# Edge attention on one core: batches of eight tiles in place of four

## The chip, the core and the metric

The kernel runs on one core of one Trainium2 chip. The core has TensorE (PE, with its weight loads PEld), VectorE (DVE), ScalarE (ACT), GpSimd (POOL) and SyncE (SP), which run at once, each through its own instructions in order. A queue instruction (SPq, ACTq, POOLq in the profile) loads registers or starts a transfer. The metric is device time in microseconds (us). Three runs of the kernel before took 2592.5, 2565.03 and 2586.32 us; the median is 2586.32 us.

## What is computed

A graph attention layer with 6250 nodes and 206250 edges, 128 features in 8 heads of 16, then a residual and a layer norm. The edges are sorted by destination.

```python
Qh = (h @ WQ).reshape(N, H, D); Kh = (h @ WK)...; Vh = (h @ WV)...
Eh = (edge_attr @ WE).reshape(-1, H, D)
score = einsum('ehd,ehd,ehd->eh', Kh[src], Qh[dst], Eh) / sqrt(16)
score = exp(clip(score, -5.0, 5.0))
wV = segment_sum(Vh[src] * score[:, :, None], dst)
Z  = segment_sum(score, dst)
x  = layernorm(x + wV / (Z[:, :, None] + 1e-06))
```

All is float32 in and out.

## The kernel before

**Tiles and batches.** 128 edges make a tile, one edge to a partition; there are NT = 1612 tiles. Four tiles make a batch (B = 4), 406 batches with the short ones at the end (`cut_batches`). The loop at L580 runs once for each batch b and issues one stage of batch b, another of b-1 and a third of b-2:

- `stage_a(b)` on PE: L464 forms Q of the batch's edges from a one-hot matrix (`onehotT`) and rows of Q, into the one `qps` buffer; L469 forms E from the edge attributes `ea` into the one `eps` buffer. Each buffer is one PSUM bank (4 x 128 floats). A buffer is free again when DVE has read it.
- `stage_b(b-1)` on DVE: `kq` = K x Q (L475), `kqe` = kq x E (L478), the sum by heads `sc` (L481), the clip (L484). Between these lie, for a batch to come, the one-hot matrices `onehot` (L437, reads `iota_p` in PSUM) and `onehotT` (L450), both made for two batches at a time, and calls of `fill`, each of which issues one instruction of the waiting layer norms or of the waiting rows of Q.
- `weigh(b-1)` on ACT: exp of the scores twice, into `exp_p` in PSUM (L490) and into the tail of `msg` (L492).
- `messages(b-2)` on DVE: msg = V x exp_p (L519).
- `stage_c(b-2)` on PE: L541 adds onehot x msg into `agg`, a window of 64 nodes; eight tiles share one window. Two windows share a PSUM tile, which ACT copies out in one piece (`sum`, L552).

**K and V by two ways.** Before the loop a table `kv` of K and V of all nodes is made. For each tile POOL starts an indirect transfer (`gather`, L397) of 128 rows of it into `kvrows`. The first transfer of batch b waits for the Q matmuls of batch b - lag(b) (L401); the rest of the batch follow it. One tile in ten takes another way instead: `columns` (L370) copies its nodes' columns of x, one after another at addresses held in registers, 96 of 128 on ACT and 32 on DVE. The addresses are loaded eight at a time from `col_at` (L365). When a column tile `xcol` is complete, PE multiplies it (L379, `colkv`) and DVE places the result (L386). On ACT a batch's copies stand in two halves, one before `weigh` and one after it; on DVE they stand behind `messages` and ahead of the clip. `COLP` sets the rate: a column tile in every 5/2 batches, from batch COL0 = 32 on, started COLL batches ahead. There are 146 such tiles and 14016 copies on ACT.

**Order.** From batch XB = 12 on the order on each engine is that of the program. SP's queue holds the loads of `ea` (8 tiles each, three such chunks ahead), of `relb`, of the rows of Q (`qw`), and the stores. The batches before 12 gather rows of x and form K and V by `project`.

Of the kernel before, what the change touches and what calls it, by code (L numbers as in the profile page):

```python
# [16 lines left out]
P = 128  # L17
N, E, D, H, DH = 6250, 206250, 128, 8, 16
NT = (E + P - 1) // P
EPAD = NT * P  # L20
B = 4
G = 4
# [6 lines left out]
CH = 8  # L29
GB = 14  # L30
XB = 12
LOCK = XB + 6
STEP = 3
GLEAD = 2
OHB = 5
# [4 lines left out]
NG = (NT + G - 1) // G  # L40
AHEAD = 2
EB = 6
SLAG = 2
WT = 8
# [6 lines left out]
QREG = 16  # L51
COL0 = 32
COLP = (5, 2)
COLA = (8, 12)
COLV = (8, 4)
COLL = 8
RING = 4096
SUMS = 8
XT_AT = RING + P
# [3 lines left out]
def cut_batches():  # L63
    out, t = [], 0
    while t < NT:
        k = B
        if t >= NT - TAIL:
            k = 2 if NT - t > 3 else 1
        out.append(range(t, t + k))
        t += k  # L70
    return out
# [30 lines left out]
def edge_attention(ctx: ExitStack, tc: tile.TileContext, x, xT, srcT, srcC, dstT, dstB, dst0, bnd, lo, eaT,  # L102
# [25 lines left out]
    ident = cp.tile([P, P], F32, name="ident")  # L128
    onehots = [cp.tile([P, HW + 2 * B * P], F32, name=f"onehot{i}") for i in range(OHB)]
    cnt_i = cp.tile([1, 1], I32, name="cnt_i")  # L130
# [10 lines left out]
    with ExitStack() as fast:  # L141
# [98 lines left out]
        psT = fast.enter_context(tc.tile_pool(name="psT", bufs=2, space=bass.MemoryType.PSUM))  # L240
        psA = fast.enter_context(tc.tile_pool(name="psA", bufs=2, space=bass.MemoryType.PSUM))
# [106 lines left out]
        used = [0]  # L348

# [58 lines left out]
        def project(g, n):  # L408

            pt = psT.tile([P, B, P], F32, name="xtps", tag="oT")  # L410
            for i in range(n):
                nc.tensor.transpose(pt[:, i, :], g[:, i, :D], ident)
            xgT = wp.tile([P, B, P], F32, name="xgT", tag="kq", bufs=2)
            nc.scalar.copy(xgT[:, :n], pt[:, :n])
            for i in range(0, n, 2):
                k = min(2, n - i)
                pk = pair_bank(i // 2, "kvps", [P, 2, 2 * D])
                for j in range(k):
                    nc.tensor.matmul(pk[:, j, :], xgT[:, i + j, :], wkv_sb, start=True, stop=True)  # L419
                nc.scalar.copy(g[:, i:i + k, :], pk[:, :k, :])  # L420

        def together(b):

            t0 = batches[b][0]
            n = len(batches[b])
            if n == B and b + 1 < nbat and len(batches[b + 1]) == B and t0 % (2 * B) == 0:
                return [b, b + 1]
            return [] if n == B and t0 % (2 * B) else [b]

        def stage_0(b):  # L430
            group = together(b)
            if not group:
                return
            t0, n = batches[b][0], sum(len(batches[i]) for i in group)
            tl = onehots[used[0] % OHB]
            used[0] += 1
# [3 lines left out]
            for i in group:  # L440
                st8[i] = tl, HW + (batches[i][0] - t0) * P - HW * pair_of(batches[i][0])[1], None

        def stage_0t(b):
            group = together(b)
            if not group:
                return
            t0, n = batches[b][0], sum(len(batches[i]) for i in group)
            ohT = wp.tile([QROWS, 2 * B * P], BF16, name="onehotT", bufs=3)
# [3 lines left out]
            for i in group:  # L452
                tl, at, _ = st8[i]
                k = (batches[i][0] - t0) * P
                st8[i] = (tl, at), ohT[:, k:k + len(batches[i]) * P]

# [15 lines left out]
        def stage_b(b):  # L472
            n, g, oh, pq, pe = st8[b]
            t0 = wp.tile([P, B, D], F32, name="kq", bufs=2)
            nc.vector.tensor_tensor(t0[:, :n], g[:, :n, :D], pq[:, :n], op=ALU.mult)  # L475
            yield
            t1 = wp.tile([P, B, D], F32, name="kqe", bufs=2)
            nc.vector.tensor_tensor(t1[:, :n], t0[:, :n], pe[:, :n], op=ALU.mult)  # L478
            yield
            sc = wp.tile([P, B, H], F32, name="sc")  # L480
            nc.vector.tensor_reduce(sc[:, :n], t1[:, :n].rearrange("p b (h d) -> p b h d", h=H),  # L481
                                    axis=AX.X, op=ALU.add)
            yield
            nc.vector.tensor_scalar(sc[:, :n], sc[:, :n], -20.0, 20.0, op0=ALU.max, op1=ALU.min)  # L484
            st8[b] = [n, g, oh, sc]

        def weigh(b):

            n, g, oh, sc = st8[b]
            nc.scalar.activation(exp_p[:, :n], sc[:, :n], AF.Exp, scale=0.25)  # L490
            m = wp.tile([P, B, MW], F32, name="msg")
            nc.scalar.activation(m[:, :n, D:], sc[:, :n], AF.Exp, scale=0.25)  # L492
# [7 lines left out]
        def add_windows(ps, q, first, stop):  # L500

            parts = windows(q)
            for i, (k, s) in enumerate(parts):
                nc.tensor.matmul(ps, shift[:, P - s:2 * P - s], sums[k // 2][:, k % 2],  # L504
                                 start=first and i == 0, stop=stop and i == len(parts) - 1)
# [18 lines left out]
        def stage_c(b):  # L524
            n, g, oh, m = st8.pop(b)
            for i in range(n):
# [6 lines left out]
                final = k == NT  # L533
                u = k if final else k // 2
                first = u not in aggs
                if first:
                    aggs[u] = psA.tile([P, 2, MW], F32, name="agg")
                    if final:
                        add_windows(aggs[u][:, 0], QL, True, False)
                tail = k == NT if t == NT - 1 else pair_of(t + 1)[0] != k  # L540
                nc.tensor.matmul(aggs[u][:, 0 if final else k % 2], oh[0][:, oh[1] + i * P:oh[1] + i * P + P], m[:, i, :],  # L541
                                 start=not final and t % (2 * G) == 0, stop=tail)
                if tail and final:
# [3 lines left out]
                    while norms:  # L547
                        fill()
                    norms.append(layernorm(nc, sp, aggs.pop(u)[:, :1], xbs.pop(QL), out, QL, 1, stores))
                elif tail and (k % 2 == 1 or t == LAST - 1):  # L550
                    sums[u] = sp.tile([P, 2, MW], F32, name="sum", bufs=SUMS)
                    nc.scalar.copy(sums[u][:, :k % 2 + 1], aggs.pop(u)[:, :k % 2 + 1])  # L552
                    while len(finished) < QL // 2 and all(v // 2 <= u for v, _ in windows(2 * len(finished) + 1)):
                        ready.append(len(finished))
                        finished.append(u)

        gathered = {b: gather(b) for b in range(2)}
        for b0 in range(0, NB, KB):
# [3 lines left out]
            for b in range(len(gathered), min(XB, nbat)):  # L562
                if (b - 2 if b < 5 else b) * KB > b0:
                    break
# [20 lines left out]
        for b in range(nbat + 3):  # L585
# [7 lines left out]
            if b < nbat:  # L593
# [4 lines left out]
                if b == min(XB, nbat - 1):  # L598
                    late_loads()
                if b == min(XB + 8, nbat - 1):  # L600
                    relative(C0, NT)
                if b == 14:
                    from_window(1)
# [38 lines left out]
            if b < nbat:  # L642
                project_columns(b + GLEAD)
                build_q(q_built(min(NJ - 1, batches[b][0] // WT + QLOOK + 2)), True)
                if not qwork and len(built) < q_built(
                        min(NJ - 1, batches[min(nbat - 1, b + 4)][0] // WT + QLOOK + 2)):
# [3 lines left out]
            if b == min(60, nbat):  # L650
                count_inside()
            if b == min(80, nbat + 1):
                inside = nc.values_load(cnt_i[0:1, 0:1], min_val=0, max_val=2 * EPAD,
# [159 lines left out]
```

## Time and profile before

The profiled execution took 2567.26 us, of which the span, from the first to the last instruction, is 2565.4 us.

| What | Value | Where from |
|---|---|---|
| Profiled execution / span | 2567.26 / 2565.4 us | result and page |
| Loads of column addresses: ACT / DVE | 1752 / 584 | the view of L365 |
| Granted TensorE clock | 0.75 | result |
| DMA | 148 GB/s on average, 380.81 MB | page, part 2 |
| First and last load of column addresses on ACT | 251.8 and 2489.9 us | the view of L365 |
| One load of eight addresses on ACT / DVE | 555 / 606 ns median | the same |
| `kqe`, `sc` (128 x 512) | 676, 672 ns each | groups by line |
| exp into `exp_p` (128 x 32) | 193 ns | the same |
| copy of two windows, `sum` (128 x 272) | 374 ns | the same |

A group's time is from an instruction's start to its end; neighbours on one engine overlap, so that a run of copies of 189 ns each starts one every 95 ns. "Idle before" is the time that the engine stood still ahead of the group, and behind it stands what ended that: an instruction of another engine, or "issue", which is idle time for which the profile shows no wait.

### The profile page before, as it was taken

Reading aid. Unit: us, or ns where it says so; the run is one execution under the profiler, and the core shown is the slowest. Engines: PE = TensorE matmul, PEld = TensorE weight load, DVE = VectorE, ACT = ScalarE, POOL = GpSimd, SP = SyncE. Lnnn points to the kernel's source line nnn. Section 1 sums busy time; section 2 is a strip of 40 time slices with the busy share of each in tenths; the row PEclk is TensorE's granted clock in tenths of the full one; section 3 lists DMA queues with packets and bytes.
Section 4 is the critical chain, followed back from the end, with each engine's and each line's share of the span. In section 5 each row is a group of like instructions: output and inputs, shape, how many; then the busy total and the mean of one; then the engine's idle time right before and its main releaser. Section 6 shows DMA issues by size and latency. Waiting matters only on the chain.

```text
span 2565.4 us, 49832 instructions
## 1 busy us (share of the span) xinstructions
PE 1624.0 (63%) x9342; PEld 1407.1 (55%) x9342; DVE 1843.5 (72%) x8070; ACT 1644.0 (64%) x15015; POOL 1396.9 (54%) x1473
## 2 busy tenths in 40 slices
PE   5656566676666666666666655667666656566665
PEld 3446555565665555555555555556556555455555
DVE  2436678878777777777767777877877777777786
ACT  1211667777776677676767767777776666776760
POOL 6446555555555455555554555555655555555564
PEclk7777777777776777776777768777876777777787
DMA  7545445645554464455444544564654455545542
GB/s 233 153 130 179 136 125 157 176 134 169 153 148 132 134 176 138 123 147 174 130 135 136 175 140 129 147 175 137 183 147 126 136 144 164 145 131 144 173 145 79
DMA packets 171028, 380.81 MB, mean 148 GB/s; under 512 B 58653, under 2 KB 84569, under 8 KB 170707
## 3 DMA queue, kind: packets, MB, share of 16 engines
q0 software_dynamic: 69584, 189.03, 25.8%
q1 hardware_dynamic: 99983, 187.46, 24.4%
q14 instruction: 244, 2.00, 0.2%
q8 instruction: 77, 1.26, 0.2%
q10 hardware_dynamic: 1140, 1.06, 0.1%
HBM read 362.61 MB, written 14.81 MB: 147 GB/s over the span
## 4 chain that ended last, share of the span: by engine, by line
ACT 46%; issue 25%; DVE 11%; PE 8%; ACTq 6%; another core or an unknown queue 3%; DMA 1%; DVEq 0%; SPq 0%
ACT xcol L370 42%; ACTq L365 6%; DVE xcol L370 2%; PE agg L541 2%; PE eps L469 2%; ACT msg L492 2%; DVE kqe L478 2%; DVE msg L519 1%; DVE kq L475 1%; PE finps L504 1%; ACT exp_p L490 1%; PE kvps L419 1%; DVE sc L481 1%; ACT sum L552 1%
## 5 line engine op out<-in xcount | busy, mean ns | idle before, releaser
L397 POOL DMA_INDIRECT kvrows<-kv,src x1418 | 1350.3, 952 | 1120.4 <-PE qps L464 420.4
L370 ACT COPY xcol<-xT_sb 128x4 uint8 x14016 | 1499.0, 189 | 573.0 <-issue 560.3
L541 PE MATMUL agg<-msg,onehot 128*128 128x136 f32 x3224 | 639.1, 358 | 441.3 <-DVE msg L519 316.8
L541 PEld LDWEIGHTS agg<-msg,onehot 128*128 128x128 f32 x3224 | 562.4, 254 | 492.2 <-ACT msg L492 276.5
L469 PE MATMUL eps<-we_sb,ea 128*128 128x128 f32 x3224 | 599.6, 343 | 164.5 <-DVE kqe L478 95.3
L469 PEld LDWEIGHTS eps<-we_sb,ea 128*128 128x128 f32 x3224 | 517.8, 244 | 220.6 <-DVE kqe L478 128.7
L519 DVE TENSOR_TENSOR msg<-kvrows,exp_p 128x512 f32<-128x512 f32 x406 | 275.9, 679 | 488.8 <-ACT exp_p L490 276.4
L370 DVE COPY xcol<-xT_sb 128x4 uint8 x4672 | 410.9, 192 | 30.2 <-issue 23.0
L464 PE MATMUL qps<-qw,onehotT 126*128 126x128 bf16 x1612 | 193.5, 254 | 240.7 <-DVE kq L475 163.2
L464 PEld LDWEIGHTS <-onehotT 126*128 126x128 bf16 x1612 | 154.7, 117 | 325.3 <-issue 306.8
L478 DVE TENSOR_TENSOR kqe<-kq,eps 128x512 f32<-128x512 f32 x406 | 274.6, 676 | 52.3 <-remote 30.7
L475 DVE TENSOR_TENSOR kq<-kvrows,qps 128x512 f32<-128x512 f32 x406 | 273.7, 674 | 37.5 <-remote 21.3
L481 DVE TENSOR_REDUCE sc<-kqe 128x32 f32<-128x512 f32 x406 | 272.8, 672 | 5.8 <-DVE y L761 0.5
L490 ACT ACTIVATE exp_p<-sc 128x32 f32<-128x32 f32 x406 | 78.3, 193 | 139.7 <-DVE sc L484 76.8
L437 DVE TENSOR_TENSOR onehot<-iota_p,dst_sb 128x512 f32<-128x512 f32 (+2 forms) x206 | 137.6, 669 | 11.0 <-remote 9.0
L379 PE MATMUL colkv<-wkv_sb,xcol 128*128 128x256 f32 x292 | 127.9, 533 | 0.0
L504 PE MATMUL finps<-sum,shift 128*128 128x136 f32 x640 | 95.2, 310 | 17.1 <-ACT sum L552 11.1
L504 PEld LDWEIGHTS finps<-sum,shift 128*128 128x128 f32 x640 | 91.1, 219 | 19.6 <-ACT sum L552 13.1
L492 ACT ACTIVATE msg<-sc 128x32 f32<-128x32 f32 x406 | 87.2, 215 | 22.2 <-issue 21.7
L450 DVE TENSOR_SCALAR onehotT<-relb,node 126x1024 bf16<-126x1024 bf16 (+2 forms) x206 | 99.8, 485 | 1.8 <-DMA relb<-relD 1.7
L484 DVE TENSOR_SCALAR sc<-sc 128x32 f32<-128x32 f32 x406 | 83.7, 206 | 4.2 <-issue 3.8
L379 PEld LDWEIGHTS colkv<-wkv_sb,xcol 128*128 128x128 f32 x292 | 69.1, 285 | 0.0
(73 smaller groups left out, 568.9 us busy)
## 6 DMA issues: line engine op xcount, KB each, us to landing
ea<-eaT SPq DMA_DIRECT2D x201, 512.0 KB
relb<-relD SPq DMA_DIRECT2D x100, 504.0 KB
kvrows<-kv,src POOLq DMA_INDIRECT x1418
qw<-qs SPq DMA_DIRECT2D x202, 31.5 KB
kv<-kvst SPq DMA_DIRECT2D x12, 512.0 KB
qs<-qst SPq DMA_DIRECT2D x48, 96.0 KB
xb<-x SPq DMA_DIRECT2D x24, 128.0 KB
out<-h SPq DMA_DIRECT2D x24, 128.0 KB
```

The source lines that it names most:

```text
L365: at = nc.values_load_multi_w_load_instructions(col_at[k % col_half:k % col_half + 1, k // col_half, j:j + size], engines=(engine,), min_v ...
L370: copy(to[:, 4 * (j + c):4 * (j + c) + 4], xT_bytes[:, ds(at[c] - XT_AT, 4)])
L379: nc.tensor.matmul(pk, col_tiles.pop(k), wkv_sb, start=True, stop=True)
L397: ins = nc.gpsimd.indirect_dma_start(out=g[:k, i, :f], out_offset=None, in_=rows, in_offset=bass.IndirectOffsetOnAxis(ap=src_col(t)[:k], a ...
L464: expanded[b] = nc.tensor.matmul(pq[:, i, :], ohT[:, i * P:i * P + P], loaded[t0 // WT], start=True, stop=True)
L469: nc.tensor.matmul(pe[:, i, :], ea[:, i * P:i * P + P], we_sb, start=True, stop=True)
L475: nc.vector.tensor_tensor(t0[:, :n], g[:, :n, :D], pq[:, :n], op=ALU.mult)
L478: nc.vector.tensor_tensor(t1[:, :n], t0[:, :n], pe[:, :n], op=ALU.mult)
L481: nc.vector.tensor_reduce(sc[:, :n], t1[:, :n].rearrange("p b (h d) -> p b h d", h=H), axis=AX.X, op=ALU.add)
L504: nc.tensor.matmul(ps, shift[:, P - s:2 * P - s], sums[k // 2][:, k % 2], start=first and i == 0, stop=stop and i == len(parts) - 1)
L519: nc.vector.tensor_tensor(m[:, :n, :D].rearrange("p b (h d) -> p b h d", h=H), g[:, :n, D:].rearrange("p b (h d) -> p b h d", h=H), exp_p[ ...
L541: nc.tensor.matmul(aggs[u][:, 0 if final else k % 2], oh[0][:, oh[1] + i * P:oh[1] + i * P + P], m[:, i, :], start=not final and t % (2 * ...
```

## The change

Eight tiles make a batch (206 batches). E and Q of a batch take two PSUM banks each, still one buffer each. To find the banks, `iota_p` and `exp_p` become two parts of one tile `bank`, and the window sums `agg` become one tile for the whole kernel, in whose two halves the windows alternate; ACT copies each window by itself (136 wide). `kqe` is written over `kq`; `sc` and `msg` have two buffers. `onehot` and `onehotT` are made for each batch by itself, which is eight tiles as before. Seven calls of `fill` stand in an iteration where four did. The gathers, the look-ahead and the column rate are scaled, a column tile falling on 6/5 batches of eight, 9.6 tiles. By the code there are 150 of them.

```diff
-B = 4
+B = 8
-GB = 14
-XB = 12
-LOCK = XB + 6
-STEP = 3
-GLEAD = 2
+GB = 8
+XB = 6
+LOCK = XB + 3
+STEP = 2
+GLEAD = 1
-AHEAD = 2
-EB = 6
-SLAG = 2
+AHEAD = 1
+EB = 5
+SLAG = 1
-COL0 = 32
-COLP = (5, 2)
+COL0 = 16
+COLP = (6, 5)
-COLL = 8
+COLL = 5
-SUMS = 8
+SUMS = 16
...
-        iota_p = psX.tile([P, HW], F32, name="iota_p")
-        exp_p = psX.tile([P, B, H], F32, name="exp_p")
+        bank = psX.tile([P, HW + B * H], F32, name="bank")
+        iota_p, exp_p = bank[:, :HW], bank[:, HW:].rearrange("p (b h) -> p b h", h=H)
+        agg = psA.tile([P, 2, MW], F32, name="agg")
...
-            return max(STEP, 12 - (b - LOCK) // 40)
+            return max(STEP, 6 - (b - LOCK) // 20)
...
-            t1 = wp.tile([P, B, D], F32, name="kqe", bufs=2)
+            t1 = t0
-            sc = wp.tile([P, B, H], F32, name="sc")
+            sc = wp.tile([P, B, H], F32, name="sc", bufs=2)
-            m = wp.tile([P, B, MW], F32, name="msg")
+            m = wp.tile([P, B, MW], F32, name="msg", bufs=2)
...
+                nc.tensor.matmul(agg[:, u % 2], oh[:, i * P + HW - HW * half:][:, :P], m[:, i, :],
                                  start=not final and t % (2 * G) == 0, stop=tail)
...
+                elif tail:
+                    sums[k] = sp.tile([P, MW], F32, name="sum", bufs=SUMS)
+                    nc.scalar.copy(sums[k], agg[:, k % 2])
...
             fill()
+            fill()
             next(steps, None)
             if b + AHEAD < nbat:
                 stage_0t(b + AHEAD)
+            fill()
             fill()
...
             if b < nbat:
                 columns(nc.vector, b)
+            fill()
             fill()
```

More of the change, by code (lines that the diff above doesn't have):

```diff
@@ L128, in edge_attention @@
     ident = cp.tile([P, P], F32, name="ident")
-    onehots = [cp.tile([P, HW + 2 * B * P], F32, name=f"onehot{i}") for i in range(OHB)]
+    onehots = [cp.tile([P, HW + B * P], F32, name=f"onehot{i}") for i in range(OHB)]
     cnt_i = cp.tile([1, 1], I32, name="cnt_i")
@@ L408, in project @@
         def project(g, n):
[L410 to L428, printed above, removed]
-        def stage_0(b):
[L431 to L436, printed above, removed]
+            for a in range(0, n, G):
+                h = min(G, n - a)
+                pt = psT.tile([P, G, P], F32, name="xtps", tag="oT")
+                for i in range(h):
+                    nc.tensor.transpose(pt[:, i, :], g[:, a + i, :D], ident)
+                xgT = wp.tile([P, G, P], F32, name="xgT", tag="kvst", bufs=2)
+                nc.scalar.copy(xgT[:, :h], pt[:, :h])
+                for i in range(0, h, 2):
+                    k = min(2, h - i)
+                    pk = pair_bank(i // 2, "kvps", [P, 2, 2 * D])
+                    for j in range(k):
+                        nc.tensor.matmul(pk[:, j, :], xgT[:, i + j, :], wkv_sb, start=True, stop=True)
+                    nc.scalar.copy(g[:, a + i:a + i + k, :], pk[:, :k, :])
+        def stage_0(b):
+            t0, n = batches[b][0], len(batches[b])
+            tl = onehots[b % OHB]
             nc.vector.tensor_tensor(tl[:, HW:].rearrange("p (t n) -> p t n", n=P)[:, :n, :HW],
@@ L439, in stage_0 @@
                                     rel[:, t0:t0 + n, None].to_broadcast([P, n, HW]), op=ALU.is_equal)
-            for i in group:
-                st8[i] = tl, HW + (batches[i][0] - t0) * P - HW * pair_of(batches[i][0])[1], None
+            st8[b] = tl, None
         def stage_0t(b):
[L444 to L448, printed above, removed]
+            t0, n = batches[b][0], len(batches[b])
+            ohT = wp.tile([QROWS, B * P], BF16, name="onehotT", bufs=2)
             e0 = t0 % RC * P
@@ L451, in stage_0t @@
                                     op0=ALU.is_equal)
[L452 to L455, printed above, removed]
+            st8[b] = st8[b][0], ohT
         def stage_a(b, g):
@@ L548, in stage_c @@
                         fill()
[L549 to L553, printed above, removed]
+                    norms.append(layernorm(nc, sp, agg[:, u % 2:u % 2 + 1], xbs.pop(QL), out, QL, 1, stores))
+                elif tail:
+                    sums[k] = sp.tile([P, MW], F32, name="sum", bufs=SUMS)
+                    nc.scalar.copy(sums[k], agg[:, k % 2])
+                    while len(finished) < QL // 2 and all(v <= k for v, _ in windows(2 * len(finished) + 1)):
                         ready.append(len(finished))
-                        finished.append(u)
-        gathered = {b: gather(b) for b in range(2)}
+                        finished.append(k)
+        gathered = {0: gather(0)}
         for b0 in range(0, NB, KB):
@@ L562, in edge_attention @@
             for b in range(len(gathered), min(XB, nbat)):
-                if (b - 2 if b < 5 else b) * KB > b0:
+                if (2 * b - 1 if b < 3 else 2 * b + 1) * KB > b0 and b0 + KB < NB:
                     break
```

31 lines of the change are left out of this document (13 added, 18 removed).

## The prediction, made before the changed kernel was run

> **What bounds the kernel now.** I read the page first: the busy times, the chain that ended last, the costliest groups.
>
> ```profile
> PE 1624.0 (63%) x9342; PEld 1407.1 (55%) x9342; DVE 1843.5 (72%) x8070; ACT 1644.0 (64%) x15015; POOL 1396.9 (54%) x1473
> ...
> ACT 46%; issue 25%; DVE 11%; PE 8%; ACTq 6%; another core or an unknown queue 3%; DMA 1%; DVEq 0%; SPq 0%
> ...
> L370 ACT COPY xcol<-xT_sb 128x4 uint8 x14016 | 1499.0, 189 | 573.0 <-issue 560.3
> ```
>
> DVE is busiest, but the chain runs through ACT: 46% ACT's own work, nearly all column copies, 25% "issue". The copies take 1499.0 us and 573.0 us of standing still ahead of them, together 2072 us of the 2238 us between ACT's first and last column load (251.8 and 2489.9). Next the view of waits: who is late?
>
> ```profile
> ACT xcol L370 <- issue: 560.3, 1033, 1.2
> DVE msg L519 <- ACT exp_p L490: 276.4, 151, 6.1
> ACT exp_p L490 <- DVE sc L484: 76.8, 22, 18.7
> ```
>
> DVE waits for ACT's exp (276.4 us), ACT for DVE's scores much less, and in the column stretch only 10.5 us. So ACT's stream of copies sets the pace there: 2238 us / 14016 = 159.7 ns a copy, everything included.
>
> **What makes ACT stand.** In the timeline ACT's idle "issue" time comes in phases, and they lie in the later part of POOL's runs of gathers. A run is a row of gathers with 0.3 us between them, 1.25 us each. The view by stages, for column copies alone, over a run of three (from 1003.08), one of four (1007.81), one of eight (1052.01 to 1061.78) and one of seven (1068.09 to 1076.66):
>
> ```profile
> core 0: us, PE busy (x) PEld busy (x) DVE busy (x) ACT busy (x), PEclk, DMA share, GB/s
> 1003.00:1006.00 3.00, 0.00 (x0) 0.00 (x0) 0.95 (x12) 2.63 (x28) 1.00 0.94 269
> 1006.00:1007.80 1.80, 0.00 (x0) 0.00 (x0) 0.54 (x7) 0.84 (x9) 1.00 0.75 189
> 1007.80:1010.80 3.00, 0.00 (x0) 0.00 (x0) 1.54 (x16) 2.84 (x30) 0.80 0.25 71
> 1010.80:1013.70 2.90, 0.00 (x0) 0.00 (x0) 0.00 (x0) 1.16 (x10) 0.50 0.42 124
> ...
> 1052.00:1055.00 3.00, 0.00 (x0) 0.00 (x0) 1.39 (x16) 2.84 (x30) 0.83 0.86 244
> 1055.00:1062.80 7.80, 0.00 (x0) 0.00 (x0) 0.00 (x0) 2.19 (x16) 0.50 0.42 123
> 1062.80:1068.10 5.30, 1.06 (x2) 0.56 (x2) 0.67 (x8) 4.34 (x45) 0.54 0.04 15
> 1068.10:1071.10 3.00, 0.00 (x0) 0.00 (x0) 1.34 (x16) 2.82 (x30) 1.00 0.23 57
> 1071.10:1077.70 6.60, 0.00 (x0) 0.00 (x0) 1.81 (x16) 1.92 (x13) 0.76 0.37 104
> ```
>
> The first 3 us of every run carry about 30 ACT copies, full rate. After that the rate falls to about 2 per us (16 in 7.8 us, 13 in 6.6 us) until 1 us after the run, and a pause of 0.9 us ahead of the run at 1052 was enough to give full rate again. The DMA share does not order these rows (0.86 in a fast one, 0.42 in the slowest). Counted over all runs from 300 to 2450 us, copies started per us, by the us since the run began: runs of four (136 of them) 9.1, 9.1, 8.4, 3.5, 3.1, 3.3; of seven (40) 9.5, 9.2, 8.6, 3.0, 3.2, 2.1, 0.4, 2.6, 1.8, 1.7, then 9.5; of eight (15) 8.7, 10.0, 9.9, 3.4, 3.1, 1.7, 0.5, 2.3, 1.7, 1.5, 1.3, 6.7, then 9.7. From the start of one run to that of the next, between 600 and 2400 us: 5.30 us after a run of three (76 cases), 6.23 of four (104), 13.96 of seven (38), 15.56 of eight (14). Two batches fetched apart take 11.5 us, fetched in one run 14 to 15.6.
>
> **The change part by part.**
>
> *Gathers.* A batch's gathers follow one trigger. Seven (eight where the batch has no column tile) will now always make one run; today this is so in 55 of 287 runs. An iteration has 14400/180 = 80 ACT copies. In five of six iterations a run of seven: 42.1 copies in 10 us by the row above, the other 37.9 at 9.5 per us, 14.0 us. In the sixth a run of eight: 50.8 copies in 12 us and 29.2 at 9.7, 15.0 us. POOL is busy 9 to 10 us of these, so the next run stays apart.
>
> *Exps and window copies on ACT.* In the timeline a pair of exps costs ACT 0.25 us from start to next start. From the exp of 32 (193 ns) to the copy of 272 (374 ns) is 0.76 ns an element, so a pair of 64 costs 0.30 and replaces two: -0.20 us an iteration. Two copies of 136 for one of 272 cost +0.07 per two iterations. Net -0.165 us, within bounds of -0.25 and 0. The iteration: (5 x 13.8 + 14.85)/6 = 14.0 us.
>
> *DVE.* No row shows these products at 1024 elements from two banks; nearest is a tensor_tensor of 128x1024 in SBUF at 1224 ns and a reduce at 1212. So kq, kqe, sc and msg save 4 x (2 x 0.675 - 1.22) = 0.5 us per eight tiles, and between 0 and 0.7; a clip less saves 0.2. It's hidden: DVE waits for ACT. The Perfetto Trace Analysis page of the Trainium skill (Optimizing Scalar/DVE Operations) says that larger operations help where the engine is saturated, and that smaller ones may be better where it isn't and makes bubbles elsewhere. By the first half of it 0.7 us an iteration would come off the end; DVE's 72% speaks for the second.
>
> *A new wait.* `iota_p` and `exp_p` now share a tile, and in the built program `onehot` waits for ACT's exp; before, only msg did. Behind it in DVE's queue stand kqe, onehotT, sc, msg, the placing, the column copies and the clip, and for the clip ACT's next exp waits. That chain by the rows: 0.67 + 1.22 + 0.49 + 1.21 + 1.22 + 0.35 + 26.7 x 0.088 + 0.21, 0.88 for layer norm and Q rows, 0.3 for the exp: 8.9 us. It runs beside ACT's 14.0, with 5 us to spare: nothing.
>
> *PE, SP, the rest.* E and Q of eight tiles wait for kq and kqe as before, half as often; PE is 63% busy and off the chain: nothing. The agg matmuls now wait for ACT's copy of the window before, which stands about 40 copies behind the exp, and msg also comes late: 0 to 2 us, on PE alone. SP's stores of Q rows hold its queue up to 30 us (its waits in 1000:1400), with `ea` loaded two chunks (28 us) ahead and SP itself running ahead: PE waited 1.8 us for `ea` in that stretch, so 0, at most some us for each of 49 stores, and PE has room. In-place kqe: no instruction more or less.
>
> *Ends.* Columns begin at tile 96 as now (252 us). The start I leave alone: same table, same 48 projected tiles, bounds -10 and +15. The last ACT copy falls in iteration 192, leaving 76 tiles where 56 take 75 us today (2490 to 2565): 102 us.
>
> Sum: 252 + 180 x 14.0 + 102 = 2874 us of span, against 252 + 2238 + 75 = 2565; with the 1.9 us around it 2876. The profiled execution (2567.26) lies 0.7% under the median of the runs; halfway gives **2890**.
>
> **Rivals.**
>
> *Run length is not the cause, faster.* Long runs and slow ACT might have a third cause. If eight tiles then cost what two short cycles do, 11.53, plus 3.2 copies more (0.3), less 0.165: 11.7 us, 252 + 2106 + 102 = 2460. For it: one long run replaces two triggers and the chain of 8.9 us would allow it. Against: the slow rows end with the run, 191 runs of both lengths agree on the first 6 us, and the idle time is no semaphore's. The Runtime: NRT & Kernel Launch page of the Trainium skill (Instruction fetch mechanics) has engines fetch their instructions by themselves, mostly hidden; by it ACT would be fed evenly and this case would hold. The 560.3 us of issue speak against it.
>
> *Issue loss goes with the number of copies, not with runs.* 14400 x 159.7 ns = 2300, less 180 x 0.165: 2270; 252 + 2270 + 102 = 2624, slower by 2%. For: ACT's program is hardly changed. Against: 11.5 and 14 us for the same work.
>
> *The new wait closes a loop on DVE, far slower.* DVE's copies fall 7 to 9 us into a run; there its steps grew from 83 to 150 to 205 ns. At 205 the chain has 12.0 us, hidden. At ACT's slow rate (0.45 us) 26.7 copies add 9.7: 18.6 us an iteration, 3700. It decides from 14.0 us on, when 14 of the copies are that slow. Against: DVE's copies stood for issue only 23 us in all.
>
> **How the numbers follow.** Forecast 0.70, its iteration 13.4 to 14.8 us, so 2770 to 3020; faster 0.12; loss by copies 0.13; the DVE loop 0.05. The range 2600 to 3030 takes in the forecast and the loss by copies and leaves out the others, and what the forecast's own spread misses. Faster by over 1%: 0.12. Within 1%, about what these runs can tell from no change: 0.04, from the edge of the loss by copies. Slower: 0.84.
>
> **What would show it.** Right: POOL's gathers in runs of seven and eight, one an iteration; an iteration near 14 us; issue ahead of ACT's copies at 900 us or more; ACT's copies at 30 in the first 3 us of a run and about 2 per us after it. Wrong: issue at 560 or less with the same runs (first rival); ACT waiting long for the clip, and DVE's onehot for the exp with DVE otherwise full (third); gathers broken into shorter runs.

## The result and the profile after

The changed kernel took 2729.73 us (median of four runs, 2725.0 to 2731.12) against 2581.77 for the kernel before beside it: a ratio of 1.0576, 95% interval 1.0515 to 1.0637, so slower by 5.8%. The forecast was 2890.

One sentence is needed to read what follows: the same kernels were run on several occasions, and on some of them, this result among them, the kernel before takes 2535 to 2593 us, on the others 1940 to 1951, so each experiment below says which of the two (a "2570 session" or a "1945 session") it ran in, and is compared only within it.

The page of the changed kernel: busy times, chain, ACT's column copies (busy, mean ns, idle before).

```profile
PE 1566.3 (57%) x9350; PEld 1428.6 (52%) x9350; DVE 1784.5 (65%) x7202; ACT 1659.2 (61%) x15099; POOL 1393.6 (51%) x1469
...
ACT 48%; issue 28%; DVE 7%; ACTq 7%; PE 4%; another core or an unknown queue 4%; POOL 1%; DMA 1%; DVEq 0%; SPq 0%; POOLq 0%
...
L370 ACT COPY xcol<-xT_sb 128x4 uint8 x14400 | 1548.3, 190 | 754.5 <-issue 745.2
```

The chain is ACT's as before. Its own work hardly changed; the standing still ahead of the copies went from 560.3 to 745.2 us. The view of waits (us in total, times, longest) adds two of the other engines:

```profile
ACT xcol L370 <- issue: 745.2, 1252, 1.8
POOL kvrows L397 <- PE qps L447: 727.6, 158, 16.2
...
DVE onehot L427 <- ACT bank L473: 351.7, 125, 11.5
```

POOL now waits for the Q matmuls at most once per batch, 158 times. DVE's `onehot` waits for ACT's exp, the wait that the shared tile made. The view of the address loads (min/median/max ns, first and last start) dates the column stretch:

```profile
L365 ACTq TENSOR_LOAD <-col_at x1800: 535/553/1667, 230.5 to 2618.5; - x180
```

2388 us for 180 loads, 13.27 us per 80 copies, where before 2238.1 us for 14016 copies make 12.77. So the 163.9 us between the two spans (2729.3 and 2565.4) are: start -21.3, stretch +149.9, end (last load to the end) 110.8 against 75.5, +35.3. Of the stretch, 61 us are the 384 copies more, at the 159.7 ns a copy of before; 89 us are the slower pace.

Where in a run does ACT stand? The view by stages for column copies alone, over two runs of seven gathers (1007.88 to 1016.3 and 1021.02 to 1029.6):

```profile
core 0: us, PE busy (x) PEld busy (x) DVE busy (x) ACT busy (x), PEclk, DMA share, GB/s
1007.80:1010.80 3.00, 0.00 (x0) 0.00 (x0) 0.00 (x0) 3.00 (x33) 1.00 0.95 294
1010.80:1012.80 2.00, 0.00 (x0) 0.00 (x0) 0.40 (x6) 1.30 (x12) 0.51 1.05 228
1012.80:1017.80 5.00, 0.00 (x0) 0.00 (x0) 1.61 (x20) 1.45 (x8) 0.50 1.01 314
1017.80:1020.80 3.00, 1.06 (x2) 0.56 (x2) 0.00 (x0) 2.88 (x29) 0.50 0.98 235
1021.00:1024.00 3.00, 0.00 (x0) 0.00 (x0) 0.00 (x0) 2.66 (x28) 0.99 0.65 202
1024.00:1026.00 2.00, 0.00 (x0) 0.00 (x0) 0.00 (x0) 1.85 (x18) 0.62 0.40 121
1026.00:1031.00 5.00, 0.32 (x1) 0.54 (x2) 2.20 (x26) 1.35 (x9) 0.50 0.39 107
```

Full rate at first, then 8 and 9 copies in 5 us, then full rate again 1.5 us after the run's last gather: the picture of before. But the full rate lasts longer. Counted over all runs of seven between 300 and 2400 us, copies started per us since the run began:

| Kernel | Runs of seven | 0 | 1 | 2 | 3 | 4 | 5 | 6 | 7 | 8 | 9 | Sum |
|---|---|---|---|---|---|---|---|---|---|---|---|---|
| before | 40 | 9.5 | 9.2 | 8.6 | 3.0 | 3.2 | 2.1 | 0.4 | 2.6 | 1.8 | 1.7 | 42.1 |
| changed | 129 | 9.6 | 9.6 | 9.7 | 8.2 | 5.3 | 2.5 | 0.7 | 2.4 | 1.9 | 1.3 | 51.2 |

Call a stall an idle time of more than 0.25 us that the profile puts down to "issue". In the long runs of before ACT's first stall comes 3.46 us after a run's start, after 36 ACT instructions (address loads counted) on average; in the changed kernel after 4.61 us and 49.

### The profile page after: what moved, and what is told of

Read it like the earlier page. It is cut to its first block, busy times and chain, and to the rows that moved or that the text cites. A ratio compares the mean times of both kernels' runs of the same rounds, so it can differ in the third digit from the quotient of the medians.

```text
span 2729.3 us, 48345 instructions
## 1 busy us (share of the span) xinstructions
PE 1566.3 (57%) x9350; PEld 1428.6 (52%) x9350; DVE 1784.5 (65%) x7202; ACT 1659.2 (61%) x15099; POOL 1393.6 (51%) x1469
## 3 DMA queue, kind: packets, MB, share of 16 engines
q10 hardware_dynamic: 1140, 1.06, 0.1%
## 4 chain that ended last, share of the span: by engine, by line
ACT 48%; issue 28%; DVE 7%; ACTq 7%; PE 4%; another core or an unknown queue 4%; POOL 1%; DMA 1%; DVEq 0%; SPq 0%; POOLq 0%
ACT xcol L370 45%; ACTq L365 7%; POOL kvrows L397 1%; DVE xcol L370 1%; DVE kq L461 1%; ACT sum L532 1%; PE eps L452 1%; PE kvps L421 1%; ACT msg L475 1%; DVE msg L502 1%; ACT bank L473 1%; DVE sc L464 1%; PE kvacc L263 1%; PE agg L521 1%
## 5 line engine op out<-in xcount | busy, mean ns | idle before, releaser
L370 ACT COPY xcol<-xT_sb 128x4 uint8 x14400 | 1548.3, 190 | 754.5 <-issue 745.2
L452 PE MATMUL eps<-we_sb,ea 128*128 128x128 f32 x3224 | 658.3, 386 | 426.1 <-DVE kq L461 339.3
L452 PEld LDWEIGHTS eps<-we_sb,ea 128*128 128x128 f32 x3224 | 606.2, 289 | 473.4 <-DVE kq L461 376.3
L521 PE MATMUL agg<-msg,onehot 128*128 128x136 f32 x3224 | 544.0, 333 | 182.1 <-remote 100.8
L427 DVE TENSOR_TENSOR onehot<-bank,dst_sb 128x512 f32<-128x512 f32 (+2 forms) x206 | 139.5, 677 | 387.5 <-ACT bank L473 351.7
L458 DVE TENSOR_TENSOR kq<-kvrows,qps 128x1024 f32<-128x1024 f32 (+2 forms) x206 | 246.4, 1196 | 65.1 <-issue 29.5
L461 DVE TENSOR_TENSOR kq<-kq,eps 128x1024 f32<-128x1024 f32 (+2 forms) x206 | 243.7, 1183 | 41.4 <-remote 37.4
L464 DVE TENSOR_REDUCE sc<-kq 128x64 f32<-128x1024 f32 (+2 forms) x206 | 244.5, 1187 | 0.2
L502 DVE TENSOR_TENSOR msg<-kvrows,bank 128x1024 f32<-128x1024 f32 (+2 forms) x206 | 244.3, 1186 | 0.3 <-ACT bank L473 0.3
L532 ACT COPY sum<-agg 128x136 f32<-128x136 f32 x201 | 52.9, 263 | 116.8 <-remote 65.8
L473 ACT ACTIVATE bank<-sc 128x64 f32<-128x64 f32 (+2 forms) x206 | 44.9, 218 | 60.2 <-DVE sc L467 50.7
L386 DVE COPY kvrows<-colkv 128x256 f32<-128x256 f32 x150 | 62.5, 416 | 0.0
```

The lines of the kernel that those rows point to most:

```text
L370: copy(to[:, 4 * (j + c):4 * (j + c) + 4], xT_bytes[:, ds(at[c] - XT_AT, 4)])
L452: nc.tensor.matmul(pe[:, i, :], ea[:, i * P:i * P + P], we_sb, start=True, stop=True)
L502: nc.vector.tensor_tensor(m[:, :n, :D].rearrange("p b (h d) -> p b h d", h=H), g[:, :n, D:].rearrange("p b (h d) -> p b h d", h=H), exp_p[ ...
L521: nc.tensor.matmul(agg[:, u % 2], oh[:, i * P + HW - HW * half:][:, :P], m[:, i, :], start=not final and t % (2 * G) == 0, stop=tail)
```

## The experiments

**The change in a 1945 session** (r1_before: the kernel before, unchanged; r2_after: the changed kernel, unchanged).

> The kernel before, unchanged, once more with a profile, since it took 1948 us beside the first four experiments and 2582 us beside the result. If the chip of those experiments feeds ACT evenly (theory A needs uneven feeding, which this chip then doesn't show): about 1948 us, issue idle ahead of ACT's copies under 100 us where it was 560, and another engine than ACT on the path, DVE by its busy share of 92% in the merged kernel.

> The changed kernel, unchanged, beside it. Theory A: where ACT is fed evenly, long gather runs cost nothing, and the change is worth what it saves on DVE, 0.5 to 0.7 us per eight tiles or 100 to 140 us, less the new wait of onehot: 1890 to 1930 us against 1948, faster by 1 to 3%. Theory B (the size of the batch itself makes it slower): slower by 5% here too, about 2050 us.

Measured: 1945.27 us, and 1907.25 against 1944.5, a ratio of 0.9815 (0.9789 to 0.984): there the change is faster by 1.9%. Page of the kernel before, then of the changed kernel:

```profile
PE 1404.6 (72%) x9342; PEld 1220.7 (63%) x9342; DVE 1798.9 (93%) x8070; ACT 1580.6 (81%) x15015; POOL 1402.2 (72%) x1473
...
L370 ACT COPY xcol<-xT_sb 128x4 uint8 x14016 | 1421.1, 190 | 68.7 <-issue 59.2
```

```profile
PE 1312.2 (69%) x9350; PEld 1197.3 (63%) x9350; DVE 1739.7 (91%) x7202; ACT 1571.6 (83%) x15099; POOL 1397.1 (73%) x1469
...
L370 ACT COPY xcol<-xT_sb 128x4 uint8 x14400 | 1448.8, 190 | 45.5 <-issue 36.3
```

One copy takes 190 ns as ever, but the 560 us of "issue" are 59. POOL has rows of up to 137 gathers without a pause there (191 in the changed kernel), and ACT does not starve. In the kernel before DVE is the bound, 93% busy and 52% of the chain that ended last, and the change takes 59 us of DVE's work away (1798.9 to 1739.7). That is the first half of the rule of the Trainium skill that the prediction weighed (Perfetto Trace Analysis, Optimizing Scalar/DVE Operations: larger operations help a saturated engine); in the session of the result, with DVE at 72%, it does not apply. So the starving in long runs is not of the kernel alone, and everything below that concerns it needs a 2570 session.

**Are the many transfers to blame?** (e7_before_pk and e8_after_pk, 1945 session: an extra transfer of 1024 elements of four bytes per four tiles, in both kernels.)

```diff
+                for _ in range(len(batches[b]) // G):
+                    small = ep.tile([P, 8], F32, name="small", bufs=6)
+                    nc.sync.dma_start(small, x[:P, 0:16:2])
```

> The kernel before with one more transfer for every four tiles, 1024 elements of 4 bytes that nothing reads, so that the core's DMA engines move some 580,000 packets in place of 171,000. It asks what makes the engines stand with issue idle where the kernel before takes 2580 us. If it is the number of packets in flight beside them (theory P): issue idle ahead of ACT's copies above 200 us, locked to stretches rich in packets, and a time above 2050 us. If packets have no part in it: issue idle 40 to 100 us as in the kernel before on this chip, time 1945 to 2000 us.

> The changed kernel with the same packets for each four tiles. Under theory P with theory A on top (long gather runs then cost more): slower than the kernel before with the same packets, by 2 to 8%. Otherwise 0.97 to 0.99 of it, as without the packets.

Measured: 1944.16 and 1914.91 us, beside 1945.8 for before. 588071 packets in place of 171028 left ACT's "issue" at 58.8 us (59.2 without them), so the number of packets alone does not starve it there. In a 2570 session this was not tried.

**Long runs in the kernel before** (e2_merge and e2_again in 1945 sessions, e2_third in a 2570 session: one edit makes an even batch's gathers wait for the same Q matmuls as the odd batch's, so that both follow in one run).

```diff
-                    made = expanded[b - lag(b)]
+                    made = expanded[b - lag(b) + (1 - b % 2)]
```

> The kernel before, batches of four, but the gathers of an even batch wait for the same Q matmuls as those of the odd batch behind it, so that POOL fetches two batches in one run. Theory A: nearly all runs of 7 and 8, 13.3 to 14.4 us per two batches, time 2690 to 2850 us. Theory B: no change, 2560 to 2600 us.

> The kernel before with two batches' gathers in one run, on another chip, since the kernel before took 2582 us beside the result and 1945 to 1948 us on two chips since. Where the kernel before takes about 2580 us here (ACT fed unevenly): theory A 2690 to 2850 us, theory B 2560 to 2600 us. Where it takes about 1946 us: the same as before, within 0.3%.

> The kernel before with two batches' gathers in one run, on one more chip. Where the kernel before takes about 2580 us: theory A 2690 to 2850 us, theory B 2560 to 2600 us. Where it takes about 1945 us: the same as before, within 0.3%.

Measured: 1948.52 us (ratio 1.0008, 0.9997 to 1.0019), 1948.21 beside 1946.4, and in the 2570 session 2811.94 beside 2557.36, one run each: 10% slower by one wait. Groups of e2_third:

```profile
L397 POOL DMA_INDIRECT kvrows<-kv,src x1418 | 1348.9, 951 | 1366.9 <-PE qps L464 950.9
L370 ACT COPY xcol<-xT_sb 128x4 uint8 x14016 | 1517.7, 190 | 757.7 <-issue 748.1
```

Between 300 and 2400 us 151 runs of seven or eight and none of three or four; "issue" 748.1 us where the same copies had 560.3. PE, DVE and ACT have the same instructions as before, and in the 1945 sessions the later trigger cost nothing, so this is the length of the runs.

**Short runs by a pause** (e12_before_rest, kernel before; e10_rest, changed kernel; both in one 2570 session). A memset on POOL, of a tile that nothing else uses, stands ahead of each batch's gathers in the one and ahead of the fifth gather of a batch in the other.

```diff
+    rest = cp.tile([P, 1536], mybir.dt.uint8, name="rest")
...
+                if i == 0 and b >= XB:          # e12_before_rest; i == G in e10_rest
+                    nc.gpsimd.memset(rest, 0)
```

> The kernel before with the same memset on POOL ahead of each batch's gathers, so that the 55 runs of seven or eight gathers come apart into runs of three and four. Theory A: 55 cycles of 14.0 to 15.6 us become two of 5.3 to 6.2 us each, 55 x 2.8 = 150 us less: 2380 to 2460 where the kernel before takes some 2560 us. Theory C: 2540 to 2590. Where the kernel before takes some 1945 us: 1930 to 1960 by both.

> The changed kernel with one GpSimd memset of 128x1536 bytes on a tile of its own between the fourth and the fifth gather of each batch (an estimate of 1 to 2 us, from the iota of 128x384 at 442 ns), so that no run of gathers on POOL is longer than four, whatever any semaphore does. Theory A (the length of an uninterrupted run of gathers is what starves the engines; in the changed kernel the first stall comes 4.62 us after the start of a run, and four gathers take 5.0 us): if the chip is one on which the kernel before takes some 2560 us, the issue idle ahead of ACT's column copies falls from 745 us to under 400, and the time lies at 2200 to 2430. Theory C (each gather costs its share of stalls, however they are grouped): 2690 to 2760. If the kernel before takes some 1945 us, both give 1890 to 1960, and the run tells nothing of the question.

Measured: 2412.53 us (one run) and 2505.72 (ratio 0.9772, 0.9668 to 0.9877) beside 2569.19: both faster than both kernels. Groups of e12_before_rest, then of e10_rest:

```profile
L371 ACT COPY xcol<-xT_sb 128x4 uint8 x14016 | 1484.1, 189 | 424.3 <-issue 410.8
```

```profile
L371 ACT COPY xcol<-xT_sb 128x4 uint8 x14400 | 1525.3, 190 | 487.7 <-issue 477.0
```

The kernel before falls into its expected range. Of the 154.7 us that its span loses (2565.4 to 2410.7), 124 lie in the column stretch (217.6 to 2331.6 us); 34 lie ahead of it, where the runs of 8 to 19 gathers that start between 129 and 216 us in the kernel before are broken up as well. The changed kernel gains 220.6 us of span and yet misses its range, which took for granted that ACT would stall as late in short runs as in long ones. Two things bear on that. With one pause per batch, 37 of 305 runs (300 to 2400 us) still have seven or eight, since a batch's last gathers run into the next batch's first. And after a pause of 1.56 us the first stall comes some 3.2 us into a short run, where in the changed kernel's long runs it came after 4.7 (medians). By the address loads the column stretch takes 12.04 us per 80 copies (233.3 to 2400.2 us), against 12.07 in e12_before_rest: with short runs batches of eight and of four go at nearly the same pace. What keeps e10_rest 98.0 us of span behind is 384 copies more (some 53 us more of stretch), a start 16 us later and an end 29 us longer.

**The new wait, taken away** (e3_iota in a 1945 session, e13_iota in a 2570 session; e6_iota12 is the first with COLP = (3, 2), fewer column tiles, in a 1945 session).

```diff
-                                    iota_p[:, None, :].to_broadcast([P, n, HW]),
+                                    iota_f[:, None, :HW].to_broadcast([P, n, HW]),
```

> The changed kernel with onehot reading the same numbers from SBUF, so that it no longer waits for ACT's exp in the shared bank. Theory C: the 352 us that onehot waits go, 2400 to 2600 us. Theory A: DVE waits for the exp at msg in its place, 2700 to 2800 us; if ACT and DVE draw on one common delivery of instructions, DVE's copies come earlier in a run, ACT gets fewer than 48 instructions ahead of its first stall, and the time rises by 0 to 3%.

> The changed kernel with onehot reading from SBUF and a column tile in every 12 tiles in place of 9.6, so that ACT and DVE copy a fifth less and POOL gathers some 30 tiles more. Where ACT is fed unevenly: 64 ACT copies an iteration, 51 in the first 10 us of a gather run and the rest at 9.3 per us, 11.4 us an iteration, 2350 to 2450 us against 2580. Where it is fed evenly: POOL is the bound of the kernel with onehot from SBUF (1414 gathers x 1.25 us = 1768 of 1892 us), so 30 gathers more cost 38 us, 1920 to 1940 us.

> The changed kernel with only the ids of onehot read from the SBUF copy (so no wait for the exponential), and the gathers as they are. Theory S (all engines draw on one delivery of instructions, and a DVE that stands at onehot leaves it to ACT): the first stall moves from 4.6 us after the start of a run back to 3.6 us, and where the kernel before takes some 2560 us this takes 2760 to 2830, as the run with the split gathers did. Rival W (that run was slow because its gathers waited for something later): 2680 to 2740 here. Where the kernel before takes some 1945 us: 1885 to 1900 by both.

Measured: 1891.25 us (ratio 0.9711, 0.9695 to 0.9727, the best of the 1945 sessions), 1936.81 beside 1946.4, and 2793.92 beside 2569.19. Without the wait the changed kernel is 16 us faster in the one kind of session (1907.25 was its own time) and 63 us slower by the span (2792.1 against 2729.3) in the other. The 63 us compare one run with the result of another 2570 session, but e9_split_iota below, with the same edit, took 2797.89. e6_iota12 lies in its range: a fifth fewer column copies and 30 gathers more made it 45.6 us slower than e3_iota. Waits and stages (one run of seven, 1026.7 to 1035.4) of e13_iota:

```profile
ACT xcol L370 <- issue: 793.6, 1408, 1.2
```

```profile
1026.70:1029.70 3.00, 0.00 (x0) 0.00 (x0) 2.37 (x27) 2.86 (x29) 1.00 0.23 63
1029.70:1031.70 2.00, 0.00 (x0) 0.00 (x0) 0.48 (x7) 0.96 (x8) 1.00 0.42 123
1031.70:1036.70 5.00, 0.59 (x2) 0.31 (x2) 0.00 (x0) 1.27 (x10) 1.00 0.37 105
```

DVE's copies now fall into the run's first 3 us, and ACT starts 8 copies in the next 2 us where the changed kernel had 12 and 18. Over 126 runs of seven the first stall comes after 3.7 us (median; 4.7 in the changed kernel), and the ten us of the table above sum to 46.7 copies. So the wait at `onehot` delays ACT's stall.

**Is it DVE's share of the instructions?** (e4_nodve in a 1945 session, e14_nodve in a 2570 session: the kernel before without DVE's 32 column copies per column tile; a memset of these columns stands in for them, and that part of K and V is left out of the output.)

```diff
+                    nc.vector.memset(col_tiles[k][:, 96:], 0.0)
...
-                columns(nc.vector, b)
+                pass
```

> The kernel before with DVE's 32 column copies and 4 loads per column tile left out, one fill of zeros in their place. If ACT and DVE draw on one common delivery (theory A with a shared stock): ACT starts 43 to 50 instructions from a run's begin to its first stall in place of 35.6, first stall at 4 us or later in place of 3.4, time 2350 to 2500 us. If each engine has its own: 35 instructions, 3.4 us, time within 1% of 2580 us, since DVE is not on the path.

> The kernel before without DVE's 32 column copies of each of its column tiles (one memset of those columns takes their place, so the output leaves that part out). Theory S: DVE issues 24 of the 65 to 70 instructions that all engines start before the first stall of a run; without its copies the stall comes later, and the issue idle ahead of ACT's column copies falls from 560 us to 300 to 450: 2300 to 2470 where the kernel before takes some 2560 us. Rival O (each engine has a delivery of its own, and ACT's share of the columns is unchanged): the issue idle stays at 530 to 590, the time at 2530 to 2590. Where the kernel before takes some 1945 us: 1875 to 1890 by both.

Measured: 1881.28 us (ratio 0.9659, 0.9643 to 0.9675), in the kind of session where DVE is the bound; and 2529.29 beside 2569.19. Waits of e14_nodve:

```profile
ACT xcol L371 <- issue: 553.9, 1075, 1.2
```

553.9 against 560.3 us. The first stall of a long run comes 3.74 us after its start (3.46 before), after 39 of ACT's instructions in place of 36, though only 10.3 of DVE's lie ahead of it where there were 24.2 (means). A stock of instructions that all engines share, which I had read from the nearly equal sums of ACT's and DVE's instructions ahead of a stall (59.8 before, 62.2 after), is refuted: the sum is 49 here. DVE's copies do seem to cost ACT something (46.8 copies in ten us of a run of seven against 42.1). How much time that is, the run doesn't show, for its gathers fell together otherwise: 71 of its 270 runs are of seven or eight, 55 of 278 before. At the 2.8 us apiece by which the expectation of e12_before_rest priced them, the 16 more are 45 us, which can hide a gain.

**A split by a semaphore** (e1_split in a 1945 session; e9_split_iota, with the edit of `onehot` too, in a 2570 session: the last four gathers of a batch wait for the last `agg` matmul of batch b - lag - 2).

```diff
+                if i == G and b >= LOCK:
+                    made = summed[b - lag(b) - 2]
-                if i == 0 and made is not None:
+                if (i == 0 or i == G and b >= LOCK) and made is not None:
...
-                nc.tensor.matmul(agg[:, u % 2], oh[:, i * P + HW - HW * half:][:, :P], m[:, i, :],
+                summed[b] = nc.tensor.matmul(agg[:, u % 2], oh[:, i * P + HW - HW * half:][:, :P], m[:, i, :],
```

> The changed kernel with each batch's gathers in two runs: the fifth gather of a batch waits for the last agg matmul of the batch two before the one whose Q matmuls release the first, some 6 us later. Theory A (the length of POOL's gather runs sets how far ACT's copies fall behind): runs of 4 and of 3 to 4 in place of 7 and 8, an iteration of 11.5 to 12.0 us, issue idle ahead of ACT's copies down from 745 to 350-500 us, time 2430 to 2530 us, below the kernel before. Theory B (the loss goes with batches of eight or with the number of copies): 2700 to 2750 us. Theory C (onehot waiting for the exp sets the iteration): 2700 us or more.

> The changed kernel with both edits at once, each batch's gathers in two runs and onehot reading from SBUF, on one more chip. Where the kernel before takes about 2580 us (uneven feed): theory A 2400 to 2520 us. Where it takes about 1945 us: 1885 to 1905 us, since with even feed the split gains nothing and the wait of onehot is worth 16 us.

Measured: 1913.48 us (ratio 0.9829, 0.9812 to 0.9845) and 2797.89 beside 2557.36, a plain miss. Its runs tell why: 145 of 157 still have seven or eight gathers, and all 145 begin at the fifth gather of a batch. POOL's waits of e9_split_iota, for the new trigger and for the old one:

```profile
POOL kvrows L397 <- PE agg L523: 715.6, 135, 8.9
...
POOL kvrows L397 <- PE qps L449: 68.8, 17, 9.5
```

POOL waits at the new trigger. By the time it comes, the old trigger of the batch behind is over, so a batch's last four gathers and the next batch's first four make one run. A wait that is already over makes no pause: the edit moved the long runs by half a batch, and the time stayed that of e13_iota (2793.92).

**Shorter pauses** (e15_before_short: a memset of 128x768 ahead of each batch; e16_after_short: one of 128x1024 ahead of the first and of the fifth gather; both drew a 1945 session).

```diff
+    rest = cp.tile([P, 768], mybir.dt.uint8, name="rest")      # 1024 in e16_after_short
...
+                if i == 0 and b >= XB:                         # i % G == 0 in e16_after_short
+                    nc.gpsimd.memset(rest, 0)
```

> The kernel before with a shorter memset on POOL ahead of each batch's gathers: 128x768 bytes, 698 ns by the 1396 ns of 128x1536, so that POOL stands still between two runs for some 0.87 us instead of 1.56. Theory A with a delivery that recovers at once: the pauses of 0.87 us do as much as those of 1.56, POOL has 394 x 0.7 = 276 us less to do, and the time lies at 2250 to 2400 where the kernel before takes some 2570 us. Rival R (a pause has to last over a microsecond, since ACT's copies come back to 8 per us only 1.0 us after a run's last gather): stalls run on from one run into the next, 2420 to 2600. Where the kernel before takes some 1945 us: POOL's own work grows from 1800 to some 2100 us, and the time is 1980 to 2150 by both.

> The changed kernel with a memset of 128x1024 bytes (930 ns by the same row, a pause of some 1.09 us) ahead of the first and ahead of the fifth gather of each batch, so that no run is longer than four; with the memset ahead of the fifth alone, 37 of 305 runs still had seven or eight, since a batch's last gathers ran into the next batch's first. Theory A: 2280 to 2450 where the kernel before takes some 2570 us, under the 2506 of one memset. Rival F (what holds the changed kernel with short runs is its own chain, not the stalls: DVE stood in 21% of the chain of waits of the run with one memset): 2450 to 2540. Where the kernel before takes some 1945 us: 1960 to 2150 by both, with POOL's work as the bound.

Measured: 2116.45 us (ratio 1.0894, 1.0872 to 1.0916) and 2196.86 (1.1299, 1.1281 to 1.1318). The first lies in its range, the second 47 us above; their questions on the length of a pause stay open, as there is no starving in such a session. What they show is the price of the pause. DVE's column copies, in the changed kernel of r2_after and in e16_after_short:

```profile
L370 DVE COPY xcol<-xT_sb 128x4 uint8 x4800 | 386.6, 192 | 11.4 <-issue 9.9
```

```profile
L371 DVE COPY xcol<-xT_sb 128x4 uint8 x4800 | 521.8, 427 | 20.7 <-issue 17.7
...
L399 POOL MEMSET rest<- 128x1024 uint8 x394 | 382.1, 970 | 0.2
```

A DVE copy that overlaps a memset takes 1252 ns on average (1066 of them), the others 192; ACT's overlapping copies take 190. I had counted the pause as POOL's cost alone.

## Why the prediction was right in kind and too large

**The bound and the cause: right, in a 2570 session.** ACT's copies set the pace, and ACT stands in the later part of POOL's runs. The change made the runs of seven and eight, 129 and 26 between 300 and 2400 us and none shorter. That the length is the cause, which the prediction only read from the timeline, is now shown from both sides: long runs alone slow the kernel before by 10% (e2_third), pauses that leave only short runs make it 6% faster (e12_before_rest), and pauses take 220.6 us from the span of the changed kernel. Length alone isn't enough, though: in the 1945 sessions runs of over a hundred gathers starved nothing. What in a long run of gathers stops the engines stays open.

**The iteration of 14.0 us: the step that failed.** It was put together from "42.1 copies in 10 us by the row above, the other 37.9 at 9.5 per us", a row of the long runs of before. The runs of the changed kernel carry 51.2. At the 13.27 us measured, 180 iterations take 2388 us in place of 2520, 132 us less. That puts the time under the 2770 to 3020 of the forecast's own spread; it still lies between 2600 and 3030, but neither the forecast nor the loss by copies (2624) meets it. About half of the 9.1 copies are tied to the wait at `onehot`, since without it 46.7 are left and the iteration is 13.61 us (232.6 to 2681.9 us for 180). How a DVE that stands there puts off ACT's stall stays open, as does the other half: e14_nodve excludes that DVE's copies use up a common stock, though without them the kernel before too has 4.7 copies more in ten us. The mistake in method is plain: a count taken under one order on DVE was carried to a kernel in which DVE's copies come 3.2 us later in the run (the first of them 4.23 us after its start against 1.06, medians over the long runs).

**The new wait: priced at nothing, was a gain.** The chain of 8.9 us stayed beside ACT's, as said (ACT waited 50.7 us in all for the clip), though the step from one of DVE's column copies to the next grew to some 190, 260 and 560 ns at 7, 8 and 9 us into a run. But "nothing" was wrong: 62.8 us in favour of the change here, some 16 us against it where DVE is the bound.

**The small terms.** Products of 1024 elements take 1183 to 1196 ns against the 1220 taken. DVE's saving is hidden here, as said, but it was priced too high: 0.7 us an iteration would be 140 us over 200 batches, and DVE's busy time fell by 59.0 (1843.5 to 1784.5). The durations of the four products and of the clip did fall by 161 us in sum (1180.6 to 1020.1); but neighbours on an engine overlap, so such a sum counts time twice. The start is 230.5 us where 252 was left alone, outside its bounds of -10 and +15, a miss of 21.5; the end is 110.8 against 102. With the iteration these make the 145 us between 2874 and the span of 2729.3. Going halfway to the median added 14 us more; the profiled run of after was as long as the others.

**The rivals.** Loss by the number of copies (2624) falls with e2_third: same copies, 254.6 us more of span than the kernel before beside it (2810.2 against 2555.6). Run length as no cause (2460) falls with the same run. The DVE loop did not close. Of the signs named, the runs of seven and eight, one a batch, and the 30 copies in their first 3 us came true (28.9). Two did not: 2 copies per us right after that (8.2 and 5.3 in the fourth and fifth us) and "issue" of 900 us (745.2).

The Runtime: NRT & Kernel Launch page of the Trainium skill (Instruction fetch mechanics) has engines fetch their instructions by themselves, mostly hidden. The 36 to 59 us of the 1945 sessions agree with it; whether the 560.3 and 745.2 us here are fetching, no run shows.

## What to carry to other kernels

Before pricing a bigger batch, look at what else the trigger of a batch starts: here, in the 2570 sessions, eight gathers in a row starved the engine that set the pace, and that outweighed every instruction saved. A rate counted from stalls holds only for the order of work it was counted in, so keep such a count as one end of the range. And a kernel's sign can turn with the session: this change was 5.8% slower where ACT starved and 1.9% faster where DVE was full, so a change of this size should be timed on more than one occasion.

## What the hardware showed that I had not expected

The same kernel took 1945 us in some sessions and 2570 in others. In the two profiles of the kernel before (r1_before, and the one ahead of the change), ACT's and DVE's instructions last the same (one of ACT's column copies 190 and 189 ns, DVE's `kqe` 676 in both), and the instruction packets took 402 and 393 ns on one DMA queue and 1099 and 1040 on another (medians). PE's matmuls of L541 last 324 and 358 ns, at a granted clock of 0.88 and 0.75. The difference lies in the idle time that the profile calls "issue". What causes it was not found. The granted clock does not order it: in the stages shown above, ACT starts 10 copies in 5 us at a clock of 1.00 (e13_iota, from 1031.70) and 29 in 3 us at 0.50 (changed kernel, from 1017.80). Nor does the chip's number in the record: chips 0 and 12 each stand with both kinds of session (whether of one machine, it doesn't say).

In a 2570 session all engines slow down together late in a run of gathers: in the changed kernel's timeline ACT, DVE and PE (its weight loads and the address loads counted) together start 20 to 25 instructions per us in the second to sixth us of a run of seven or eight and 4.8 in the tenth, and ACT's full rate is back 1.5 us after the last gather.

A memset of bytes on POOL holds up DVE. In the timeline of e12_before_rest (start, us), two of DVE's instructions and the memset:

```profile
1005.60 2.25 DVE L766 TENSOR_SCALAR h<-h,mv,y 128x128 f32<-128x128 f32 x1
...
1006.36 1.40 POOL L399 MEMSET rest<- 128x1536 uint8 x1
1007.42 0.69 DVE L522 TENSOR_TENSOR msg<-kvrows,exp_p 128x512 f32<-128x512 f32 x1
```

The 128x128 operation takes 346 ns in the median of its 49 cases; here it lasts until the memset is over. The `msg` that starts during the memset takes its usual 0.69 us, and ACT's copies stay at 190 ns. The SBUF — State Buffer page of the Trainium skill (SBUF: two separate sides) has DVE and GpSimd share one pair of ports: a GpSimd instruction, or a DVE instruction of certain kinds, holds it from start to end, and the other is blocked. Copies of 1252 instead of 192 ns agree with it, and so does ACT's independence; but by the recorded starts the operation above was there 0.76 us before the memset and was held all the same. A pause that leaves SBUF alone was not tried.
